# A graph layer on Trainium2: larger buffers for decoded counts and gathered rows, loads released by runs of six blocks, and counts copied out of PSUM by pairs of banks

## The chip, the cores and the metric

The kernel runs on one core of one Trainium2 chip. The metric is the device time of one execution in microseconds (us), as the median of several. Engines are named as in the profile: PE is TensorE (PEld are its weight loads, which run beside its products), DVE is VectorE, ACT is ScalarE, POOL is GpSimd, SP is SyncE, which here only issues DMAs. PSUM has eight banks of 2 KB per partition; a bank holds 512 columns of float32.

## The reference

A layer of a graph network with pre-normalization: 12500 nodes of 128 features, 200000 edges of four types, sorted by destination.

```python
h = maximum(layernorm(x), 0)                       # [12500, 128]
for i in range(4):
    msgs += where(edge_type == i, h[src] @ W[i] + b[i], 0)
out = x + segment_sum(msgs, dst, num_segments=12500)
```

The destinations are drawn as 12500 u² with u uniform, so low-numbered nodes have many edges and high-numbered ones few.

## The kernel before, in words

The edges lie in 1563 chunks of 128. Because matrix products are linear, rows of `h` are first added up by destination and type, and the sums are multiplied by `W` afterwards. The kernel does this adding in two ways.

**The dense side** takes the first 568 chunks, whose destinations have many edges. It does not fetch a row for each edge but counts, for a small set of destinations and types (a *unit*), how often each of the 12500 source nodes occurs, and multiplies the counts with the whole table of `h`. There are 580 units in 19 batches (22 in the first batch, 31 in each other).

- `count` builds one-hot matrices on DVE (L1068, L1076) and multiplies them on PE (L1101) into `pt`, one bank of the PSUM pool `x_ps` (four banks, L278 to L281 has the PSUM pools). When the last product of a unit is issued, the copy of `pt` to SBUF as int32 (`counts`, ACT, L1109) is put on the list `owed`; `settle(owed)` issues it, at the end of the next unit at the latest. Counts of three destinations are packed into the digits of one number.
- `multiply` takes the counts of the batch before through the table `dtab` in DRAM. The table is read in 33 parts of three blocks of 128 rows (288 KB each, SP, L1200, tiles `hs`, pool of STREAM = 5). Two parts (RUN = 2), six blocks, make a *run*. In a run six products take the undecoded counts (`c = 0`, L1215) and six take decoded ones (`c = 1`, L1207); the decoding is done by ACT (L1169) into tiles `dec` of three blocks, four of them (DECS = 4). All products of a batch add up in one bank `pa`. After each three products the generator yields. The first batch goes another way (L1226, L1237) and writes `dtab` (`keep`, L1183 to L1185).
- At the end of a batch ACT reads `pa` into `sd` (L1253), `tail` multiplies it with `W` (L1260, a bank of `x_ps`), and DVE adds the result to `acc` (L1279).

**The gather side** takes the other 995 chunks, in groups of 16. POOL fetches the 128 rows of a chunk by an indirect DMA (L590) into tiles `hm` of two chunks (HG = 2, pool `rows` of 10). DVE makes a one-hot matrix for each chunk (L608), `sum_up` adds rows by destination and type on PE (L643, three products a chunk, four chunks in one bank of `s_ps`, which has two), and ACT copies such a sum to `sb` (L633, put on the list `sums_owed` and issued when the next bank of `s_ps` is taken). Then `weigh` counts the edges for the bias with four products into `pc` (L660, a bank of `x_ps`), copies them (ACT, `cnt`, L664), and multiplies `cnt` and `sb` with the weights into `py` (L667, L669, pool `y_ps` of one); DVE adds `py` to a ring of results (L732). `prep_steps` prepares indices of 128 chunks with two transposes into `pg` (L375, L376), and `leave` (L765, L770) transposes results, adds x and writes them out.

**Order.** The main loop (L1561 to L1666) goes over the groups. In it PE, DVE and ACT run in the order in which the program writes their instructions; SP and POOL are ordered by their own queues. A group has eight parts of two chunks. After each part of `sum_up`, `pace` says how much of the dense work is due, and the loop takes so many steps of `dense_work`, which mixes `count` of batch n with `multiply` of batch n−1. At the second part the `py` step of the group before is issued, at the sixth the `pc` step of this group, and at other points steps of preparation and output. After the dense work is over (`dense_out`) the loop finishes the last groups and the output.

In PSUM, `x_ps` has four banks, `s_ps` two, `y_ps` one and `a_ps` (for `pa`) one: all eight.

Of the kernel before, what the change touches and what calls it, by code (L numbers as in the profile page):

```python
# [35 lines left out]
F32 = mybir.dt.float32  # L36
# [14 lines left out]
P = 128  # L51
EPS = 1e-5
UN = 3
G = 16
# [15 lines left out]
OT = 4  # L70
HG = 2
RAW = 3
LEAD = RAW
# [3 lines left out]
DS = 3  # L77
DECS = 4
RUN = 2
UP = 4096.0  # L80
# [7 lines left out]
def kernel(  # L88
# [189 lines left out]
    x_ps = mid.enter_context(tc.tile_pool(name="x_ps", bufs=4, space=PSUM))  # L278
    s_ps = mid.enter_context(tc.tile_pool(name="s_ps", bufs=2, space=PSUM))
    y_ps = mid.enter_context(tc.tile_pool(name="y_ps", bufs=1, space=PSUM))  # L280
    a_ps = mid.enter_context(tc.tile_pool(name="a_ps", bufs=1, space=PSUM))  # L281
    raw_room = ExitStack()
    aheads = raw_room.enter_context(tc.tile_pool(name="aheads", bufs=4))
# [233 lines left out]
    NU = len(spans)  # L517

    def load_span(u):
        j0, j1 = spans[u]  # L520
        xt = hpool.tile([P, HG * D3], F16, name="hm").bitcast(F32).rearrange("p (j d) -> p j d", d=D)
        load_nodes(xt, j0, j1)
        return xt
# [60 lines left out]
    def gather(t0, g):  # L584
        got = []
        for h0 in range(0, g, HG):
            hm = hpool.tile([P, HG * D3], F16, name="hm")
            for i in range(h0, min(h0 + HG, g)):
                at = (t0 + i) % (TURN * P)
                one = nc.gpsimd.indirect_dma_start(  # L590
                    out=hm[:, (i - h0) * D3 : (i - h0 + 1) * D3],
                    out_offset=None,
                    in_=htab,
                    in_offset=bass.IndirectOffsetOnAxis(ap=srcf[:, at : at + 1], axis=0),
                )
# [4 lines left out]
        return lambda i, c: of(got[i // HG], c)[:, (i % HG * 3 + c) * D : (i % HG * 3 + c + 1) * D]  # L600

# [13 lines left out]
    def settle(of):  # L615
        while of:
            of.pop(0)()

    adds = []
# [29 lines left out]
    def weigh(t0, g, oh, sb, last):  # L649
        win = window_of(C0 + t0)  # L650

        def bank(own):
            settle(owed)
            to = y_ps.tile([P, G * WIN], F32, name="py") if own else x_ps.tile([P, G * WIN], F32, name="pt")
# [10 lines left out]
        yield True  # L665
        py = bank(not last)
        nc.tensor.matmul(py[:, :g, :], b128, cnt[:, :g, :], start=True, stop=False)  # L667
# [88 lines left out]
    def leave(j0, j1, of, c0):  # L756

        nf = min(j1, N // P) - j0
        xt = seen_out.pop(j0) if j0 in seen_out else fetch(j0, j1)
        settle(owed)  # L760
        pt = x_ps.tile([P, OT, DO], F32, name="pt")
        for j in range(j0, j1):
# [12 lines left out]

        return rest

# [69 lines left out]
    def check_all():  # L847
# [4 lines left out]
        nc.vector.tensor_copy(many[:, 2:3], held)  # L852
        pb = x_ps.tile([P, 3], F32, name="pt")
        ones = outp.tile([P, P], F32, name="ones", bufs=1)
# [189 lines left out]
    def count(now, room):  # L1044
# [6 lines left out]
        order = sorted((n / len(of), i) for of in like.values() for n, i in enumerate(of))  # L1051
        for _, i in order:
            of = slots_of(vs[i])
# [37 lines left out]
        yield 0.0  # L1091
        counts = now[1] = room().tile([P, NW + 1, UB * NT], I32, name="counts")
        for n, of in enumerate(sets):
            supply(n)
            for k, (i, s, by, first, last) in enumerate(of):
# [3 lines left out]
                if first:  # L1099
                    pb = x_ps.tile([P, NB + NT], F32, name="pt")  # L1100
                one = nc.tensor.matmul(pb, o1, o2, start=first, stop=last)  # L1101
# [4 lines left out]
                if last:  # L1106
                    settle(owed)
                    owed.append(
                        lambda i=i, pb=pb: nc.scalar.copy(  # L1109
                            counts[:, :, i * NT : (i + 1) * NT], pb.rearrange("p (b t) -> p b t", t=NT)  # L1110
                        )
                    )
                done += 1
# [37 lines left out]
    def multiply(now):  # L1151
# [9 lines left out]
        parts = [(j0, min(j0 + HB, NW)) for j0 in range(0, NW, HB)]  # L1161
        decoded = {}

        def decode(n):
            j0, j1 = n * DS, min(n * DS + DS, NW)
            if first or j0 >= NW:
                return
            decoded[n] = decp.tile([P, DS, 3 * UB * NT], F32R, name="dec")
            nc.scalar.activation(  # L1169
# [8 lines left out]
        def keep(n, hs):  # L1178
            j0, j1 = parts[n]
            both = decp.tile([P, DS, 3 * UB * NT], F32R, name="dec").rearrange("p j v -> p (j v)")  # L1180
            both = both[:, : HB * D3 // 2].rearrange("p (j f) -> p j f", j=HB)[:, : j1 - j0]
# [12 lines left out]
        pa = a_ps.tile([P, 512], F32, name="pa")  # L1194
        to = pa[:, :nv]
        for n in range(0, 0 if first else len(parts), RUN):
            run = []
            for j0, j1 in parts[n : n + RUN]:
                hs = rooms[2].tile([P, HB, D3], F16, name="hs")
                nc.sync.dma_start(hs[:, : j1 - j0, :], table[:, j0:j1, :])  # L1200
                run += [(j, hs[:, j - j0, :]) for j in range(j0, j1)]
            for c in (0, 1):
                if n + RUN + c not in decoded:
                    decode(n + RUN + c)
                for j, row in run:
                    if c:
                        nc.tensor.matmul(  # L1207
                            to.rearrange("p (m v) -> p m v", m=3),
# [3 lines left out]
                            stop=(j == NW - 1),  # L1212
                        )
                    else:
# [41 lines left out]
        def tail(sd):  # L1256
            settle(owed)
            py = x_ps.tile([P, 3 * UB], F32, name="pt")
            for t in range(NT):
# [21 lines left out]

            tails.append(rest)

# [277 lines left out]
    for gi, (t0, g) in list(enumerate(zip(starts, sizes)))[RAW:]:  # L1561
# [56 lines left out]
        if work is None and not dense_out:  # L1618
# [178 lines left out]
```

## Time and profile before

| | |
|---|---|
| median of three runs | 1589.8 us (1585.2, 1589.8, 1591.06) |
| profiled execution | 1605.82 us, span 1604.1 us |
| granted PE clock, mean | 0.930 |
| busy: PE, ACT, DVE, POOL | 1317.4, 1077.8, 1004.4, 966.3 us |
| moved by DMA | 322.55 MB, 201 GB/s in the mean |
| count copies (L1109) | 580, 278.8 us |
| decodes (L1169) | 594, 662.2 us |
| gathers (L590) | 947, 915.0 us |

A row of a group reads: line, engine, operation, tile written <- tiles read, shapes, how many; then busy time in us and the mean of one in ns; then the idle time of the engine just before these instructions, and what ended it. A row of the timeline has start and duration in us; instructions of one line that follow each other closely are one row with their number (x6). In brackets stands the idle time before, and its releaser. "SPq" rows are DMA issues, "issue" is waiting for nothing that the profile shows, "remote" for something it cannot name. A row of the waits has who waited, the tile and line, for what, then the total in us, how many times, and the longest.

### The profile page before, as it was taken

What the parts mean: (1) busy time and instruction counts of PE and PEld (TensorE: products, weight loads), DVE (VectorE), ACT (ScalarE), POOL (GpSimd) and SP (SyncE); (2) the same over time, 40 slices, a digit from 0 to 9 for tenths busy, and PEclk for the clock granted to TensorE, in tenths of its full rate; (3) what the DMA queues carried; (4) which work ended last, traced back from release to release, by engine and by line L of the source; (5) the groups of instructions that cost most, each with busy time, mean ns of one, the idle gap of its engine ahead of it and who ended that gap; (6) DMA issues with size and microseconds to landing.
All of it is one profiled execution on the core that took longest, in us unless ns stands there. A gap on an engine that the chain in (4) does not pass through costs nothing.

```text
span 1604.1 us, 30332 instructions
## 1 busy us (share of the span) xinstructions
PE 1317.4 (82%) x9232; PEld 899.3 (56%) x9232; DVE 1004.4 (63%) x5138; ACT 1077.8 (67%) x1815; POOL 966.3 (60%) x1024
## 2 busy tenths in 40 slices
PE   4876876688889887988889888888888888888885
PEld 1334654466566665656556565665656565565654
DVE  7784466647677765766665575656656565666524
ACT  5675433577677776777677776877777777767651
POOL 6525566666666666666666665666666666666662
PEclk9885798799999999999999999999999999999997
DMA  7542398476676666667676765766666666656762
GB/s 210 186 168 69 113 294 279 123 240 216 192 219 211 216 200 204 209 206 225 190 228 207 227 212 183 229 200 213 216 215 201 207 207 202 215 187 209 254 190 74
DMA packets 184629, 322.55 MB, mean 201 GB/s; under 512 B 30243, under 2 KB 82524, under 8 KB 184460
## 3 DMA queue, kind: packets, MB, share of 16 engines
q1 hardware_dynamic: 132716, 214.63, 42.1%
q0 software_dynamic: 46992, 96.30, 20.0%
q10 hardware_dynamic: 4752, 9.64, 1.6%
q8 instruction: 73, 1.20, 0.3%
q14 instruction: 96, 0.79, 0.1%
HBM read 294.78 MB, written 25.67 MB: 200 GB/s over the span
## 4 chain that ended last, share of the span: by engine, by line
PE 64%; issue 10%; DMA 8%; ACT 7%; DVE 6%; another core or an unknown queue 4%; SPq 1%; DVEq 0%; ACTq 0%
PE pa L1207 16%; PE pa L1215 15%; PE pt L1101 10%; DMA hs<-dtab 7%; PE py L669 6%; PE ps L643 6%; ACT dec L1169 3%; PE pt L1260 2%; PE pa L1237 1%; ACT counts L1109 1%; DVE o L1068 1%; PE ps L701 1%; DVE o L1076 1%; DVE ring L732 1%
## 5 line engine op out<-in xcount | busy, mean ns | idle before, releaser
L590 POOL DMA_INDIRECT hm<-htab,srcT x947 | 915.0, 966 | 570.0 <-issue 207.0
L1169 ACT ACTIVATE dec<-counts 128x1116 fp32r<-128x1116 uint8 (+1 forms) x594 | 662.2, 1136 | 46.4 <-PE pa L1207 12.6
L1068 DVE TENSOR_SCALAR o<-iota_n,hkT 128x392 bf16<-128x392 f16 x1069 | 354.3, 331 | 387.1 <-PE pt L1101 184.6
L1215 PE MATMUL pa<-counts,hs 128*128 128x372 fp8e4 x1764 | 370.9, 336 | 80.6 <-DMA hs<-dtab 37.1
L1207 PE MATMUL pa<-dec,hs 128*128 128x372 f32 x1764 | 411.9, 364 | 29.6 <-ACT dec L1169 14.9
L1109 ACT CAST counts<-pt 128x396 int32<-128x396 f32 x580 | 278.8, 496 | 184.4 <-PE pt L1101 43.7
L1207 PEld LDWEIGHTS pa<-dec,hs 128*128 128x128 f32 x1764 | 309.0, 193 | 68.7 <-issue 30.1
L1101 PE MATMUL pt<-o,o 128*128 128x396 bf16 x1069 | 292.8, 344 | 53.7 <-issue 27.0
L1215 PEld LDWEIGHTS <-hs 128*128 128x128 f16 x1764 | 160.2, 99 | 234.4 <-issue 81.3
L1076 DVE TENSOR_SCALAR o<-iota_b,loT,byT 128x128 bf16<-128x128 bf16 x647 | 213.4, 330 | 0.0
L643 PE MATMUL ps<-oh,hm 128*128 128x72 bf16 (+7 forms) x2841 | 185.0, 201 | 26.6 <-issue 20.6
L643 PEld LDWEIGHTS <-hm 128*128 128x128 f16 x2841 | 149.4, 101 | 101.9 <-issue 54.4
L732 DVE TENSOR_TENSOR ring<-ring,py 128x18 f32 (+6 forms) x912 | 158.6, 174 | 58.4 <-issue 19.3
L608 DVE TENSOR_SCALAR oh<-iota_b,keyT 128x72 bf16<-128x72 bf16 (+7 forms) x947 | 161.8, 257 | 39.3 <-PE pa L1207 23.4
L633 ACT ACTIVATE sb<-ps 128x288 f32<-128x288 f32 (+8 forms) x237 | 99.5, 421 | 108.0 <-PE ps L643 32.2
L1101 PEld LDWEIGHTS <-o 128*128 128x128 bf16 x1069 | 86.6, 99 | 84.6 <-issue 31.2
L669 PE MATMUL py<-sb,wsb 128*128 128x288 f32 (+6 forms) x456 | 123.6, 414 | 0.8 <-issue 0.8
L1076 DVE TENSOR_SCALAR o<-iota_b,loT 128x128 bf16<-128x128 bf16 x422 | 121.7, 288 | 0.0
L669 PEld LDWEIGHTS py<-sb,wsb 128*128 128x128 f32 x456 | 84.1, 195 | 25.0 <-issue 3.9
L664 ACT CAST cnt<-pt 128x288 bf16<-128x288 f32 (+10 forms) x62 | 24.3, 393 | 96.8 <-remote 38.7
L574 POOL DMA_INDIRECT hx<-in_x_dram,srcT x48 | 46.1, 961 | 39.9 <-DVE varr L493 11.0
L1237 PE MATMUL pa<-counts,hs 128*128 128x264 fp8e4 x294 | 45.8, 300 | 11.9 <-DMA hs<-htab 7.1
(251 smaller groups left out, 804.1 us busy)
## 6 DMA issues: line engine op xcount, KB each, us to landing
hs<-dtab SPq DMA_DIRECT2D x576, 288.0 KB
hm<-htab,srcT POOLq DMA_INDIRECT x947
htab<-h SPq DMA_DIRECT2D x32, 288.0 KB
hs<-htab SPq DMA_DIRECT2D x32, 288.0 KB
dtab<-dec ACTq DMA_DIRECT2D x32, 288.0 KB
xo<-in_x_dram SPq DMA_DIRECT2D x23, 256.0 KB
out_dram<-xo SPq DMA_DIRECT2D x23, 256.0 KB
hm<-in_x_dram SPq DMA_DIRECT2D x18, 192.0 KB
```

What stands on the lines that cost most here:

```text
L590: one = nc.gpsimd.indirect_dma_start(out=hm[:, (i - h0) * D3 : (i - h0 + 1) * D3], out_offset=None, in_=htab, in_offset=bass.IndirectOffse ...
L608: nc.vector.tensor_scalar(oh[:, i, :], iota_b[:, :K], keyf[:, at : at + 1], None, ALU.is_equal)
L643: nc.tensor.matmul(ps[:, i - i0, :], rows(i, c), oh[:, i, :], start=(c == 0), stop=(c == 2))
L669: nc.tensor.matmul(py[:, :g, :], wsb[:, t, :], sb[0][:, :g, t, :], start=False, stop=(t == NT - 1))
L732: nc.vector.tensor_tensor(to, to, of(i), ALU.add)
L1068: one = nc.vector.tensor_scalar(o2[:, k, :NB], iota_n, hkT[:, s : s + 1], None, ALU.is_equal)
L1076: one = nc.vector.tensor_scalar(o1[:, k], iota_b, loT[:, s : s + 1], by, ALU.is_equal, ALU.mult)
L1101: one = nc.tensor.matmul(pb, o1, o2, start=first, stop=last)
L1109: lambda i=i, pb=pb: nc.scalar.copy(counts[:, :, i * NT : (i + 1) * NT], pb.rearrange("p (b t) -> p b t", t=NT))
L1169: nc.scalar.activation(decoded[n][:, : j1 - j0, :nv].rearrange("p j (m v) -> p j m v", m=3), by_digit[:, j0:j1, : nu * NT * 4].rearrange(" ...
L1207: nc.tensor.matmul(to.rearrange("p (m v) -> p m v", m=3), row.bitcast(F32R)[:, D // 2 :], decoded[j // DS][:, j % DS, :nv].rearrange("p (m ...
L1215: nc.tensor.matmul(to.rearrange("p (m v) -> p m v", m=3), row[:, :D], counts[:, j, : nu * NT * 4].rearrange("p (v m) -> p m v", m=4)[:, :3 ...
```

## The change

- Gathered rows: tiles `hm` hold four chunks (HU = 4) instead of two, and the pool has 5 tiles instead of 10. The gates that hold a gather back stay at every second chunk. `load_span`, used in the set-up, puts two spans into one tile.
- Decoded counts: a `dec` tile holds a run of six blocks, and there are two (DECS // RUN) instead of four; `half(n)` gives the half for part n, to `decode` and to `keep`.
- Table loads: the load of part n+i is held by the last `c = 1` product of the run in which the load five before it (STREAM) is used.
- Count copies: after the set-up the four single banks of `x_ps` are given up for `z_ps`, two tiles of two banks each. Two units are counted into one tile, one into each bank, and `keep_pair` copies both with one ACT instruction; a unit left over at a batch's end is copied alone.
- `pair()` hands out such a tile; it first issues every copy that is on `owed` and every reader that is on the new list `unadded`. `tail`, `pg` of `prep_steps` and, until `dense_out`, `leave` take a pair and use its first bank.
- `pc` takes its bank from `bank()`: until `dense_out` that is a bank of `s_ps`, after `settle(sums_owed)`. After `dense_out` the pairs are given up for four single banks again.
- The constant AHEAD is added and not used.

The diff without the parts that only rename:

```diff
-    hpool = mid.enter_context(tc.tile_pool(name="rows", bufs=10))
+    hpool = mid.enter_context(tc.tile_pool(name="rows", bufs=5))
...
-        settle(owed)
-        pg = x_ps.tile([P, 2, P], F32, name="pt")
+        pg = (bank() if dense_out else pair()[:, 0, :])[:, : 2 * P].rearrange("p (q e) -> p q e", q=2)
...
-        for h0 in range(0, g, HG):
-            hm = hpool.tile([P, HG * D3], F16, name="hm")
-            for i in range(h0, min(h0 + HG, g)):
+        for h0 in range(0, g, HU):
+            hm = hpool.tile([P, HU * D3], F16, name="hm")
+            for i in range(h0, min(h0 + HU, g)):
...
-                if i == h0 and gates and t0 + i >= SOON:
+                if i % HG == 0 and gates and t0 + i >= SOON:
...
+    unadded = []
+
+    def pair():
+        settle(owed)
+        settle(unadded)
+        return z_ps.tile([P, 2, 512], F32, name="pz")
+
+    def bank():
+        if dense_out:
+            return x_ps.tile([P, 512], F32, name="pt")
+        settle(sums_owed)
+        return s_ps.tile([P, 512], F32, name="ps")
...
-        pc = bank(False)
+        pc = bank_of(False)
...
+        def keep_pair(pz, us):
+            to = counts.rearrange("p b (i t) -> p i b t", t=NT)
+            to = to[:, us[0] : us[-1] + 1 : max(1, us[-1] - us[0])]
+            nc.scalar.copy(to, pz[:, : len(us), : NB + NT].rearrange("p m (b t) -> p m b t", t=NT))
...
                 if first:
-                    pb = x_ps.tile([P, NB + NT], F32, name="pt")
+                    m = place[i]
+                    if m % 2 == 0:
+                        two = [pair(), sorted(order[m : m + 2])]
+                    pb = two[0][:, two[1].index(i), : NB + NT]
...
-                    owed.append(
-                        lambda i=i, pb=pb: nc.scalar.copy(
-                            counts[:, :, i * NT : (i + 1) * NT], pb.rearrange("p (b t) -> p b t", t=NT)
-                        )
-                    )
+                    if m % 2 or m + 1 == len(order):
+                        owed.append(lambda two=two: keep_pair(*two))
...
+        def half(n):
+            if n % RUN == 0:
+                twin[:] = [decp.tile([P, RUN * DS, 3 * UB * NT], F32R, name="dec")]
+            return twin[0][:, n % RUN * DS : (n % RUN + 1) * DS, :]
...
-                nc.sync.dma_start(hs[:, : j1 - j0, :], table[:, j0:j1, :])
+                load = nc.sync.dma_start(hs[:, : j1 - j0, :], table[:, j0:j1, :])
+                by = (n + i - STREAM) // RUN
+                if by in last:
+                    held_by(load, last[by], "a run of blocks is multiplied as a whole")
...
-            settle(owed)
-            py = x_ps.tile([P, 3 * UB], F32, name="pt")
+            py = pair()[:, 0, : 3 * UB]
...
-            tails.append(rest)
+            unadded.append(rest)
+            tails.append(lambda: settle(unadded))
...
+    ahead_ps.close()
+    z_ps = ahead_ps.enter_context(tc.tile_pool(name="z_ps", bufs=2, space=PSUM))
...
-    decp = counting.enter_context(tc.tile_pool(name="decp", bufs=DECS, side="right"))
+    decp = counting.enter_context(tc.tile_pool(name="decp", bufs=DECS // RUN, side="right"))
...
             counting.close()
+            ahead_ps.close()
+            x_ps = ahead_ps.enter_context(tc.tile_pool(name="x2_ps", bufs=4, space=PSUM))
```

More of the change, by code (lines that the diff above doesn't have):

```diff
@@ L71 @@
 HG = 2
+HU = 4
 RAW = 3
@@ L78 @@
 DECS = 4
+AHEAD = 3
 RUN = 2
@@ L281 @@
     a_ps = mid.enter_context(tc.tile_pool(name="a_ps", bufs=1, space=PSUM))
+    ahead_ps = mid.enter_context(ExitStack())
+    x_ps = ahead_ps.enter_context(tc.tile_pool(name="x_ps", bufs=4, space=PSUM))
     raw_room = ExitStack()
@@ L517 @@
     NU = len(spans)
+    wide = []
     def load_span(u):
         j0, j1 = spans[u]
-        xt = hpool.tile([P, HG * D3], F16, name="hm").bitcast(F32).rearrange("p (j d) -> p j d", d=D)
+        if u % 2 == 0:
+            wide[:] = [hpool.tile([P, HU * D3], F16, name="hm").bitcast(F32).rearrange("p (u j d) -> p u j d", u=2, d=D)]
+        xt = wide[0][:, u % 2]
         load_nodes(xt, j0, j1)
@@ L650, in weigh, with bank_of @@
         win = window_of(C0 + t0)
-        def bank(own):
-            settle(owed)
-            to = y_ps.tile([P, G * WIN], F32, name="py") if own else x_ps.tile([P, G * WIN], F32, name="pt")
+        def bank_of(own):
+            to = y_ps.tile([P, G * WIN], F32, name="py") if own else bank()
             return to[:, : G * win].rearrange("p (g n) -> p g n", g=G)
         ohv = oh.rearrange("p g (t n) -> p g t n", t=NT)
-        pc = bank(False)
+        pc = bank_of(False)
         for t in range(NT):
@@ L665, in weigh @@
         yield True
-        py = bank(not last)
+        py = bank_of(not last)
         nc.tensor.matmul(py[:, :g, :], b128, cnt[:, :g, :], start=True, stop=False)
@@ L759, in leave @@
         xt = seen_out.pop(j0) if j0 in seen_out else fetch(j0, j1)
-        settle(owed)
-        pt = x_ps.tile([P, OT, DO], F32, name="pt")
+        pt = (bank() if dense_out else pair()[:, 0, :]).rearrange("p (j o) -> p j o", o=DO)
         for j in range(j0, j1):
@@ L774, in rest @@
                 nc.sync.dma_start(out[(j1 - 1) * P :, :], xt[: rows_of(j1 - 1), nf, :])
-        return rest
+        if dense_out:
+            return rest
+        todo = [rest]
+        unadded.append(lambda: settle(todo))
+        return lambda: settle(todo)
     def put_out(j0, j1, again):
@@ L852, in check_all @@
         nc.vector.tensor_copy(many[:, 2:3], held)
-        pb = x_ps.tile([P, 3], F32, name="pt")
+        pb = bank()[:, :3]
         ones = outp.tile([P, P], F32, name="ones", bufs=1)
@@ L1051, in count @@
         order = sorted((n / len(of), i) for of in like.values() for n, i in enumerate(of))
-        for _, i in order:
+        order = [i for _, i in order]
+        place = {i: m for m, i in enumerate(order)}
+        for i in order:
             of = slots_of(vs[i])
@@ L1167, in decode @@
                 return
-            decoded[n] = decp.tile([P, DS, 3 * UB * NT], F32R, name="dec")
+            decoded[n] = half(n)
             nc.scalar.activation(
@@ L1179, in keep @@
             j0, j1 = parts[n]
-            both = decp.tile([P, DS, 3 * UB * NT], F32R, name="dec").rearrange("p j v -> p (j v)")
+            both = half(n).rearrange("p j v -> p (j v)")
             both = both[:, : HB * D3 // 2].rearrange("p (j f) -> p j f", j=HB)[:, : j1 - j0]
@@ L1195, in multiply @@
         to = pa[:, :nv]
+        last = {}
         for n in range(0, 0 if first else len(parts), RUN):
             run = []
-            for j0, j1 in parts[n : n + RUN]:
+            for i, (j0, j1) in enumerate(parts[n : n + RUN]):
                 hs = rooms[2].tile([P, HB, D3], F16, name="hs")
-                nc.sync.dma_start(hs[:, : j1 - j0, :], table[:, j0:j1, :])
+                load = nc.sync.dma_start(hs[:, : j1 - j0, :], table[:, j0:j1, :])
+                by = (n + i - STREAM) // RUN
+                if by in last:
+                    held_by(load, last[by], "a run of blocks is multiplied as a whole")
                 run += [(j, hs[:, j - j0, :]) for j in range(j0, j1)]
@@ L1206, in multiply @@
                     if c:
-                        nc.tensor.matmul(
+                        last[n // RUN] = nc.tensor.matmul(
                             to.rearrange("p (m v) -> p m v", m=3),
@@ L1212, in multiply @@
                             stop=(j == NW - 1),
-                        )
+                        ).ins
                     else:
```

5 lines of the change are left out of this document (2 added, 3 removed).

## The prediction, made before the changed kernel had run

> **What bounds the kernel now.** I read the page's busy shares first, then the chain, then a table of windows, and last the waits.
>
> ```profile
> span 1604.1 us, 30332 instructions
> PE 1317.4 (82%) x9232; PEld 899.3 (56%) x9232; DVE 1004.4 (63%) x5138; ACT 1077.8 (67%) x1815; POOL 966.3 (60%) x1024
> ...
> PE 64%; issue 10%; DMA 8%; ACT 7%; DVE 6%; another core or an unknown queue 4%; SPq 1%; DVEq 0%; ACTq 0%
> PE pa L1207 16%; PE pa L1215 15%; PE pt L1101 10%; DMA hs<-dtab 7%; PE py L669 6%; PE ps L643 6%; ACT dec L1169 3%; PE pt L1260 2%; PE pa L1237 1%; ACT counts L1109 1%; DVE o L1068 1%; PE ps L701 1%; DVE o L1076 1%; DVE ring L732 1%
> ```
>
> ```profile
> 400.00:600.00 200.00, 174.75 (x1277) 122.88 (x1277) 138.68 (x717) 145.40 (x228) 125.02 (x130) 0.95 0.66 208
> ...
> sum 1000.00, PE 866.38 PEld 600.84 DVE 639.80 ACT 733.98 POOL 623.65; mean PE 173.28 PEld 120.17 DVE 127.96 ACT 146.80 POOL 124.73
> ```
>
> The first of five equal windows and the sum and mean of all five: from 400 to 1400 us the work is even, PE is busy 87% of the time, ACT 73%, POOL 62%. So PE sets the pace, in one written order, and what is left to win or lose is its 134 us of idle time in those 1000: short stops at which PE waits for a table load, for ACT, or for another engine.
>
> ```profile
> PEld L1215 <- DMA hs<-dtab: 64.2, 60, 2.8
> PE pt L1101 <- ACT counts L1109: 6.4, 4, 4.1
> PE pa L1215 <- DMA hs<-dtab: 37.1, 39, 2.4
> PEld pa L1207 <- ACT dec L1169: 24.6, 30, 3.0
> PE pa L1207 <- ACT dec L1169: 14.9, 20, 2.6
> ACT dec L1169 <- PE pa L1207: 12.6, 12, 2.2
> ```
>
> (Who waited, for what: us in total, times, longest. PEld and PE show the same stop twice, in part.) Table loads cost most; the count copies, of which the change makes most, cost PE four waits. The change adds no arithmetic to PE, so its effect is in such waits.
>
> **The change, part by part.** I sum against the profiled execution (1605.82 us, 1.0% above the median of 1589.8), and carry the difference over to the median.
>
> *1. Counts copied by pairs of banks.* 580 units are copied one by one now; after, 281 pairs and 18 single ones, 299 copies.
>
> ```profile
> L1109 ACT CAST counts<-pt 128x396 int32<-128x396 f32 x580 | 278.8, 496 | 184.4 <-PE pt L1101 43.7
> L633 ACT ACTIVATE sb<-ps 128x288 f32<-128x288 f32 x36 | 15.0, 417 | 15.6 <-PE pt L1101 4.7 <-PE py L669 4.7 <-PE ps L643 3.5
> L633 ACT ACTIVATE sb<-ps 128x384 f32<-128x384 f32 x28 | 13.8, 492 | 11.2 <-PE ps L643 4.4 <-PE pt L1101 2.6 <-PE py L669 1.6
> ...
> 924.12 0.88 ACT L1109 CAST counts<-pt 128x396 int32<-128x396 f32 x2 [1.64 <-PE pt L1101]
> ```
>
> No copy of 792 columns exists before. The two L633 forms differ by 75 ns over 96 columns, 0.78 ns a column, so a pair takes 496 + 396 x 0.78 = 805 ns. Against two copies apart (992) this saves 0.19 us, against two back to back (0.88) 0.07: 281 x that is 20 to 53 us of ACT. ACT is idle over a quarter of the time, and the PE waits on ACT listed above come to some 46 us; a lighter ACT can shorten those only in part. I take -16, ends 0 and -53, nearer to the small end because the chain gives these copies 1%. The Trainium skill (Perfetto Trace Analysis, section "Optimizing Scalar/DVE Operations") says that grouping pays when the engine is saturated, and that where it is not, but makes others wait, breaking instructions up may let work finish sooner. The windows show ACT unsaturated; by that rule the -16 falls away and the sum below would be 1674.
>
> *2. Slack of those banks.* Today four banks turn, so a bank's copy may take until four units later; with two pairs the copy of a pair begins when the second unit is counted and must be done two units on. It ends 0.31 us (805 - 496) later than the second unit's copy did. If every pair showed this, 281 x 0.31 = 87 us; if none, 0. The present row (4 waits in 580) is nearest to none: +8.
>
> *3. Others that take a pair.* 19 `tail`s, 7 transposes `pg` and 19 `leave`s, 45 in all, now occupy a pair, and each allocation first issues every copy that is owed; the next count pair finds both pairs just used. The trace's own example of PE going PE to ACT and back without slack is the end of a batch, where `pa` must be read into `sd` (L1253) before the next batch's first L1215:
>
> ```profile
> 916.08 0.61 PE L1207 MATMUL pa<-dec,hs 128*128 128x372 f32 x2
> 919.70 0.48 ACT L1253 ACTIVATE sd<-pa 128x372 f32<-128x372 f32 x1
> 920.23 1.15 PE L1215 MATMUL pa<-counts,hs 128*128 128x372 fp8e4 x6 [1.07 <-ACT dec L1169]
> ```
>
> The last product ends at 916.69, ACT reads 3.0 us later, PE goes on at 920.23 after 1.07 us of idleness (it had other work for the rest). 45 x 1.07 = 48 us is the high end, 0 the low one; most of these have two pairs' time, so +5.
>
> *4. `pc` in the banks of the sums.* The counts of edges (`pc`, L660, 4 matmuls a group) leave the four single banks and take one of the two `ps` banks. Order of PSUM in a group: sum 1 in A, 2 in B, 3 in A, `pc` in B, sum 4 in A. So sum 4 (L643) waits for the copy of sum 3 (L633), which `bank()` issues immediately ahead of `pc`. Today `pc` has a bank of its own, sum 4 takes the other `ps` bank, free since long, and the copy of sum 3 comes on ACT right behind `cnt` (L664). Where ACT stands at that moment is seen in the trace:
>
> ```profile
> 910.29 0.43 PE L660 MATMUL pt<-oh,three 128*32 128x288 bf16 x4
> 910.77 0.40 ACT L664 CAST cnt<-pt 128x288 bf16<-128x288 f32 x1 [1.18 <-PE pt L660]
> ...
> 933.24 0.31 PE L660 MATMUL pt<-oh,three 128*32 128x288 bf16 x4
> 935.72 0.41 ACT L664 CAST cnt<-pt 128x288 bf16<-128x288 f32 x1
> ...
> 1082.21 0.32 PE L660 MATMUL pt<-oh,three 128*32 128x320 bf16 x4
> 1085.76 0.43 ACT L664 CAST cnt<-pt 128x320 bf16<-128x320 f32 x1
> ...
> 1105.62 0.32 PE L660 MATMUL pt<-oh,three 128*32 128x320 bf16 x4
> 1110.72 0.45 ACT L664 CAST cnt<-pt 128x320 bf16<-128x320 f32 x1
> ```
>
> In the first group ACT had waited for `pc`, so the copy would be over by 910.01: no stall. In the others ACT comes free (no idle time in front of `cnt`) 2.2, 3.2 and 4.8 us after `pc` ended, and a copy of 0.42 comes on top: 2.6, 3.6, 5.2 us that PE would stand, with the counts, the products and everything else queued behind sum 4. The same subtraction over the 57 groups up to the last decode,
>
> ```profile
> 169.22 0.35 PE L660 MATMUL pt<-oh,three 128*32 128x192 bf16 x4
> 169.92 0.34 ACT L664 CAST cnt<-pt 128x192 bf16<-128x192 f32 x1
> ...
> 1548.21 0.35 PE L660 MATMUL pt<-oh,three 128*32 128x384 bf16 x4
> 1552.71 0.48 ACT L664 CAST cnt<-pt 128x384 bf16<-128x384 f32 x1 [4.31 <-remote]
> ```
>
> (the first and the last) gives a median of 2.2 us and 126 us in all. A stop lets ACT and the loads get ahead, so later stops shrink; the round trip without slack that the trace does have costs 1.07. I take 57 x 1.07 = +61, ends 0 and +126. This is the largest term, and it is a wait on PE where none is now.
>
> *5. Loads tied to ends of six blocks.* A table load (L1200) waits for the room of a load five back. Today the first load of a run is released after 3 products of L1207, the second after 6; after, both by the sixth, three matmuls later.
>
> ```profile
> SPq L1200 <- PE pa L1207: 294.9, 117, 7.0
> ...
> 914.16 1.32 PE L1207 MATMUL pa<-dec,hs 128*128 128x372 f32 x6
> 924.51 0.83 SPq L1200 DMA_DIRECT2D hs<-dtab  x2
> 928.57 0.83 SPq L1200 DMA_DIRECT2D hs<-dtab  x2
> ```
>
> SP is mostly waiting (for L1207 alone 295 us) and issues the loads in twos already, every 4.06 us here. Six products take 1.32 us, the first three half of it, so the earlier release is lost by about 0.6 us, one load in two. The 39 to 60 stops on `hs` would each grow by that: 23 to 36 us; 288 runs x 0.6 = 173 is the far end, 0 the near one, because step 4's stops give loads time. What stands behind a held load on SP (loads of x and of indices) waits as long, none with a PE wait above. I take +8.
>
> *6. Decoded counts in one tile of six blocks.* The first decode of a run waits for six products of the run before last instead of three, 0.6 us later again; ACT waits for that 12 times now. Ends 0 and 2 x 12.6 = 25; +2.
>
> *7. Gathered rows by four chunks.* Same room, fewer releases; the last rows of a tile come free up to two chunks later.
>
> ```profile
> L590 POOL DMA_INDIRECT hm<-htab,srcT x947 | 915.0, 966 | 570.0 <-issue 207.0
> 905.78 0.94 POOL L590 DMA_INDIRECT hm<-htab,srcT  x1 [0.30 <-issue]
> PE ps L643 <- DMA hm<-htab,srcT: 0.9, 2, 0.5
> ```
>
> A gather with its issue is 1.24 us, 16 of them 20 us, a group lasts 23 (`pc` at 910.29 and at 933.24), and PE waited for rows twice: the idle time of POOL covers it, 0. Without that cover, two chunks a group at 1.24 us would be at most 2.5 x 57 = 141; nothing speaks for it. Fewer updates of semaphores by PE come with steps 1, 5 and 7 (281, about 288 and about 237 fewer).
>
> ```profile
> L1215 PE MATMUL pa<-counts,hs x1764: 325/326/535, 298.1 to 1551.4; 128*128 128x372 fp8e4 x196
> L1207 PE MATMUL pa<-dec,hs x1764: 325/333/775, 300.2 to 1554.6; 128*128 128x372 f32 x196
> ```
>
> L1207 carries such an update at every third product, L1215 hardly any; the medians differ by 7 ns, 1764 x 7 = 12 us in all. I take 0, the other end -12. The Trainium skill (TensorE: Matmul & The Clock Gate, section "The cost: per-tile semaphore tail") has increments of packed tiles one after another at about 26 ns each; an estimate by it, 806 x 26 ns, would be -21 and the sum 1637. No run here shows that.
>
> Sum: -16 + 8 + 5 + 61 + 8 + 2 + 0 = +68, so 1605.8 + 68 = 1674 for a profiled execution, and 1589.8 + 68 = **1658** for the median.
>
> **The rivals.**
> - *Faster: the new stops come out of old ones.* PE is idle 134 us in 1000 anyway, and the 126 us of step 4 use ACT's present place, which itself is late in places because PE has just run ahead. If after a stop ACT and the loads are ahead, the table waits shrink by as much, and ACT's 20 to 53 us are left: middle -30, **1560**. It decides where, with the terms of steps 2, 3, 5 and 6 at their zero ends, the round trip costs under 0.4 us net a group: 22 of the 30 us over 57 groups, 8 us being 0.5%. For: one of the four groups shown would not stop. Against: three would, by over 2 us, and the `hs` waits are not caused by ACT.
> - *No change:* the stops of step 4 are hidden too, and the +7 of the other terms is all that is left, less than can be told, **1590** to 1597.
> - *Slower by the loads:* step 4 is hidden, but the tie holds: stops on `hs` at a third of the 288 runs grow by 0.6 us, 58 us, less 16: **1632**. For: these waits are PE's costliest. Against: the rows show loads going in twos already.
>
> **How the numbers follow.** My forecast, 0.53, with its own range 1620 to 1720 (half of the round trip to most of the 126). Faster 0.28; no change 0.07; by the loads 0.12. A change under 0.5% can't be told here, the three runs of before lie 0.4% apart. Slower: 0.53 + 0.12 = 0.65. The range must reach down into the faster case: from 1552 (the far ends of step 1 and of the updates, below it, are left out, some 0.1) to 1725 (step 4 at its high end with +9 for the rest; above it some 0.08).
>
> **What would show it.** In the profile after, a row PE `ps` waiting for ACT `sb` of 40 to 130 us shows step 4 (no such row is among the longer waits now); without it my forecast is wrong. 299 count copies near 0.8 us show step 1; PE waiting for ACT counts above 20 us would show that step 2 or 3 is undersized; waits for `hs` above 130 us (64.2 and 37.1 now) step 5; PE waiting for gathered rows step 7. If ACT's idle time grows while PE's falls, the faster rival was right.

## The result: 3.3% slower, and the profile after

The median of five runs is 1653.88 us (1632.46 to 1662.95) against 1589.8 us before. The ratio leaves out two slow runs (1658.49 and 1662.95 us) and is therefore smaller than the quotient of these medians. It is 1.0334, with a 95% interval of 1.0269 to 1.0398, or about +53 us. The profiled execution took 1653.88 us, 48 us more than the one of before.

The page of the changed kernel: busy shares, the first part of its chain by line, and the groups of the count copies and of the count products.

```profile
span 1652.2 us, 29542 instructions
...
PE 1317.1 (80%) x9232; PEld 922.9 (56%) x9232; DVE 1003.3 (61%) x5138; ACT 1065.4 (64%) x1534; POOL 969.4 (59%) x1024
...
PE 62%; ACT 11%; issue 8%; DMA 6%; another core or an unknown queue 5%; DVE 5%; POOL 1%; SPq 1%; ACTq 0%; DVEq 0%; POOLq 0%
...
L1133 PE MATMUL pz<-o,o 128*128 128x396 bf16 x1069 | 304.7, 355 | 94.6 <-ACT counts L1120 50.3
...
L1120 ACT CAST counts<-pz 128x792 int32<-128x792 f32 (+1 forms) x299 | 238.4, 799 | 140.6 <-PE pz L1133 64.0
```

PE and ACT do the same work as before or less: PE 1317.1 us against 1317.4, ACT 1065.4 against 1077.8. The span grew by idle time alone. The mean granted clock was lower, 0.907 against 0.930, but two products of one line follow each other as before (in both traces 165 ns from start to start in the median with undecoded counts, 171 ns with decoded ones), so the clock is not what made the difference. In the chain ACT went from 7% to 11%, DMA from 8% to 6%: the chain now runs over ACT more often. The waits show where (line 662 is the sum of gathered rows, 652 its copy, 1133 the counts, 1120 their copies, 1254 and 1246 the products with undecoded and decoded counts, 1298 the tail, 1204 the decoding):

```profile
PE ps L662 <- ACT sb L652: 52.2, 28, 6.4
PE pz L1133 <- ACT counts L1120: 50.3, 30, 5.2
PEld L1254 <- DMA hs<-dtab: 41.8, 35, 2.7
ACT dec L1204 <- PE pa L1246: 39.6, 37, 3.4
PE pa L1254 <- DMA hs<-dtab: 27.7, 27, 2.3
PEld pz L1298 <- ACT counts L1120: 19.3, 8, 5.7
PE pz L1298 <- ACT counts L1120: 16.1, 5, 5.0
```

Three new stops of PE for ACT stand here: the fourth sum for the copy of the third (52.2 us), counts for count copies (6.4 before, 50.3 now), tails for count copies. Against that the stops for table loads fell (64.2 and 37.1 before, 41.8 and 27.7 now), and the rows of PE waiting for decoded counts (24.6 and 14.9 before) are not among the longer waits any more.

To compare kernels I summed in each trace by how much the start of one PE instruction follows the start of the one before it later than their usual spacing (gaps over 60 ns, from 300 us to the last product with decoded counts), by kind of instruction:

```
gaps of PE, us         before  after  e1_pc_only  e3_singles  e4_releases
all                     323.1  371.0       323.3       351.9        341.5
fourth sums of groups     5.5   90.8       128.7        85.8          5.2
counts, for ACT or DVE   36.6   61.2        17.5        31.0         36.5
tails, for ACT            1.2   13.3         0.9         0.9          0.7
c = 0, for table loads   71.8   43.5        33.4        77.8        102.1
c = 1, for ACT           27.6    5.8         6.6         6.3         12.0
```

All gaps grew by 47.9 us, as much as the two profiled executions differ. The parts do not add up in a simple way: 85 us of new stops at the sums came, and 50 us of old ones at the table loads and decoded counts went. The row of the fourth sums has all gaps there, also those that the view of waits puts down to something other than ACT. And the execution traced of before, 1605.82 us, lies 16 us above the median of its own runs and 22 us above the one beside e1 to e4. Differences from its column are uncertain by about as much.

### The profile page after: what moved, and what is told of

Its sections match the earlier page's. It is cut to its first block, busy times and chain, and to the rows that moved or that the text cites. A ratio compares the mean times of both kernels' runs of the same rounds, so it can differ in the third digit from the quotient of the medians.

```text
span 1652.2 us, 29542 instructions
## 1 busy us (share of the span) xinstructions
PE 1317.1 (80%) x9232; PEld 922.9 (56%) x9232; DVE 1003.3 (61%) x5138; ACT 1065.4 (64%) x1534; POOL 969.4 (59%) x1024
## 4 chain that ended last, share of the span: by engine, by line
PE 62%; ACT 11%; issue 8%; DMA 6%; another core or an unknown queue 5%; DVE 5%; POOL 1%; SPq 1%; ACTq 0%; DVEq 0%; POOLq 0%
PE pa L1246 16%; PE pa L1254 14%; PE pz L1133 11%; PE py L687 6%; PE ps L662 5%; ACT dec L1204 5%; DMA hs<-dtab 4%; ACT counts L1120 3%; PE pz L1298 2%; PE pt L975 1%; POOL hm L596 1%; PE pa L1276 1%; PE ps L678 1%; ACT sb L652 1%
## 5 line engine op out<-in xcount | busy, mean ns | idle before, releaser
L1246 PE MATMUL pa<-dec,hs 128*128 128x372 f32 x1764 | 416.3, 371 | 6.9 <-issue 3.9
L1254 PE MATMUL pa<-counts,hs 128*128 128x372 fp8e4 x1764 | 366.1, 338 | 40.9 <-DMA hs<-dtab 27.7
L1133 PE MATMUL pz<-o,o 128*128 128x396 bf16 x1069 | 304.7, 355 | 94.6 <-ACT counts L1120 50.3
L1246 PEld LDWEIGHTS pa<-dec,hs 128*128 128x128 f32 x1764 | 322.2, 200 | 33.3 <-issue 14.7
L1120 ACT CAST counts<-pz 128x792 int32<-128x792 f32 (+1 forms) x299 | 238.4, 799 | 140.6 <-PE pz L1133 64.0
L1254 PEld LDWEIGHTS <-hs 128*128 128x128 f16 x1764 | 166.0, 100 | 213.8 <-issue 78.7
L662 PE MATMUL ps<-oh,hm 128*128 128x72 bf16 (+7 forms) x2841 | 183.0, 203 | 87.8 <-ACT sb L652 52.2
L662 PEld LDWEIGHTS <-hm 128*128 128x128 f16 x2841 | 154.5, 102 | 155.7 <-issue 109.8
L1099 DVE TENSOR_SCALAR o<-iota_b,loT 128x128 bf16<-128x128 bf16 x422 | 117.4, 278 | 0.0
L682 ACT CAST cnt<-ps 128x288 bf16<-128x288 f32 (+7 forms) x58 | 23.0, 396 | 43.7 <-remote 19.6
```

Source lines behind the costliest of these rows:

```text
L662: nc.tensor.matmul(ps[:, i - i0, :], rows(i, c), oh[:, i, :], start=(c == 0), stop=(c == 2))
L1099: one = nc.vector.tensor_scalar(o1[:, k], iota_b, loT[:, s : s + 1], by, ALU.is_equal, ALU.mult)
L1120: nc.scalar.copy(to, pz[:, : len(us), : NB + NT].rearrange("p m (b t) -> p m b t", t=NT))
L1246: last[n // RUN] = nc.tensor.matmul(to.rearrange("p (m v) -> p m v", m=3), row.bitcast(F32R)[:, D // 2 :], decoded[j // DS][:, j % DS, :nv ...
L1254: nc.tensor.matmul(to.rearrange("p (m v) -> p m v", m=3), row[:, :D], counts[:, j, : nu * NT * 4].rearrange("p (v m) -> p m v", m=4)[:, :3 ...
```

## The experiments

The kernel before ran beside each of these on the same chip, and each ratio is against that. Beside e1 to e4 it took 1583.8 us; beside e5 to e8 it took 1346.6 us and beside e9 to e12 1347.8 us, the same kernel on another, faster chip. What differs there is told in the last section. The trace of before that this document shows comes from a run at 1606 us; its time places it with the slower chip, so it is set beside traces of that chip only.

### e1: the edge counts alone

```diff
             settle(owed)
+            if not own and not dense_out:
+                settle(sums_owed)
+                return s_ps.tile([P, 512], F32, name="ps")[:, : G * win]...
             to = ... if own else x_ps.tile([P, G * WIN], F32, name="pt")
```

(In the kernel before, nothing else changed. It still issues the owed count copies ahead of `pc`, by `settle(owed)`; the changed kernel no longer does so there, so its stop at the sums need not be as long as here.)

> The kernel before with one edit: the edge counts `pc` take a bank of the sums, everything else (single count copies in four banks, releases, buffers) as before. My theory: the fourth sum of a group waits for the copy of the third, so this alone costs +55 to +85 us, 1645 to 1675, and the row PE `ps` waiting for ACT `sb` shows 50 us or more. Rival, the pairs of banks cost most and this stop is absorbed: under +20, 1590 to 1610. Rival, table loads: no change, 1590.

Measured: 1594.96 us, ratio 1.0076 (1.0049 to 1.0104), about +12 us. The waits of this run (643 the sums, 1218 and 1210 the products):

```profile
PE ps L643 <- ACT sb L633: 81.3, 29, 5.8
PE ps L643 <- DMA hm<-htab,srcT: 17.5, 8, 3.8
PEld L1218 <- DMA hs<-dtab: 28.2, 32, 2.2
PE pa L1218 <- DMA hs<-dtab: 14.9, 16, 1.8
PE pa L1210 <- ACT dec L1172: 4.7, 8, 1.6
```

The stop is there: 81.3 us by this view, and by the table of gaps 123 us more ahead of the fourth sums, near the high end of the prediction (126); of these the view puts 17.5 us down to gathered rows. But the time rose by 12 us. The stops for table loads fell from 37.1 to 14.9 us and those for decoded counts from 14.9 to 4.7, and all gaps of PE together are what they were (323). That fits this account: while PE stands for one thing, the loads and ACT get ahead, and PE does not stand for them afterwards. The price is shown by the times; where the stops went rests on one pair of traces, and loads also went out less late in this one than in that of before (last section). My theory of +55 to +85 us falls: the stop came, and its price did not.

### e2: the copy of the third sum issued earlier

```diff
                 if spent is None:
                     work = None
+                if j == max(0, parts - 3) and not dense_out:
+                    settle(sums_owed)
```

> The changed kernel with one edit: the copy of a group's third sum is issued after the first dense step of its part, so that it stands on ACT about 3 us ahead of `pc`. My theory: most of the wait of the fourth sum goes, 60 us or so of the 64, and what the pairs cost (some 13) and their lighter ACT are left: 1590 to 1615. Rival, pairs: at most -20 us against the changed kernel, 1635 or more. A third way: ACT now stands and waits for the third sum and delays decodes, so that half is given back: 1615 to 1635.

Measured: 1639.85 us, ratio 1.0328 (1.0267 to 1.0389), not to be told from the changed kernel's 1.0334.

```profile
PE ps L662 <- ACT sb L652: 14.1, 12, 2.2
PEld L1254 <- DMA hs<-dtab: 62.8, 58, 3.9
PE pz L1133 <- ACT counts L1120: 47.5, 29, 5.7
PE pa L1254 <- DMA hs<-dtab: 37.2, 40, 3.3
```

The stop at the sums shrank from 52.2 to 14.1 us, and the waits for table loads rose from 27.7 to 37.2 (PE) and from 41.8 to 62.8 (weight loads). This is the same exchange as in e1, the other way round: taking most of this stop away bought nothing that can be told, where my theory had 1590 to 1615 us. The 1635 or more of the rival (pairs) came, but this run does not show that the pairs are the reason.

### e3 and e11: the pairs undone

```diff
-    z_ps = ...tile_pool(name="z_ps", bufs=2, space=PSUM)
+    z_ps = ...tile_pool(name="z_ps", bufs=4, space=PSUM)
...
-        return z_ps.tile([P, 2, 512], F32, name="pz")
+        return z_ps.tile([P, 1, 512], F32, name="pz")
...
-                    if m % 2 == 0:
-                        two = [pair(), sorted(order[m : m + 2])]
+                    two = [z_ps.tile([P, 1, 512], F32, name="pz"), [i]]
...
-                    if m % 2 or m + 1 == len(order):
-                        owed.append(lambda two=two: keep_pair(*two))
+                    owed.append(lambda two=two: keep_pair(*two))
```

(In the changed kernel; the readers of tails and outputs are issued as before, too.)

> The changed kernel with the pairs undone: each unit in a bank of its own out of four, copied by itself, tails and transposes in one bank; `pc` in the sums' banks, tied loads, larger buffers stay. My theory: the pairs' net is small (terms +8, +5, -16), so the time stays within 20 us of the changed kernel, 1635 to 1675. Rival, pairs cost most: near 1600.

Measured: 1627.57 us, ratio 1.0226 (1.0123 to 1.0329), which overlaps with the changed kernel's. So it was run again on the faster chip, beside the changed kernel itself (e9).

> The changed kernel with the pairs undone, as before (single banks, single copies; pc, ties and buffers as changed), beside the changed kernel itself. Theory: the pairs cost more by their shorter slack than their lighter ACT gives: 10 to 25 us under the changed kernel on the slower chip, 0 to 10 on the faster. Rival, prediction: pairs give about 3 us net, so it is 0 to 5 us above the changed kernel.

Measured: 1375.87 us, ratio 1.0197 (1.0162 to 1.0232), against 1388.81 and 1.0294 (1.0261 to 1.0328) for the changed kernel: the intervals lie apart, and the pairs cost 12.9 us, 1.0%. The waits of e11, and then of e9:

```profile
PE pz L1128 <- ACT counts L1116: 5.0, 5, 1.2
```

```profile
PE pz L1133 <- ACT counts L1120: 21.0, 24, 1.4
PE pz L1298 <- ACT counts L1120: 3.3, 7, 0.9
```

The difference in these rows, 16 us for the counts and some 2 for the tails, is about the price. ACT has 13 us less to do with pairs, 1054.9 us in e9 against 1067.9 in e11, and the kernel is slower all the same. First e9, then e11:

```profile
PE 1238.4 (89%) x9232; PEld 882.4 (63%) x9232; DVE 999.3 (72%) x5138; ACT 1054.9 (76%) x1534; POOL 972.6 (70%) x1024
```

```profile
PE 1229.5 (89%) x9232; PEld 881.2 (64%) x9232; DVE 995.5 (72%) x5138; ACT 1067.9 (78%) x1815; POOL 975.8 (71%) x1024
```

The rival (pairs) is right in sign here; by size it is a third of the whole.

### e4: the three releases, without the changes in PSUM

The kernel before with the tied loads, the tiles of six blocks and the rows by four, each as in the diff of the change.

> The kernel before with the releases alone: tied table loads, decoded counts in tiles of six blocks, gathered rows in tiles of four chunks; PSUM and copies as before. My theory: terms +8, +2 and 0, so 1590 to 1610. Rival, the tied loads cost most: +40 or more, 1630 and up, with the waits for `hs` grown by 30 us. Rival, fewer updates by PE help: 1565 to 1580.

Measured: 1613.11 us, ratio 1.0176 (1.0128 to 1.0225), about +28 us.

```profile
PEld L1230 <- DMA hs<-dtab: 116.8, 88, 3.3
PE pa L1230 <- DMA hs<-dtab: 79.5, 64, 2.9
ACT dec L1180 <- PE pa L1222: 25.8, 23, 2.8
```

The stops for table loads doubled, 37.1 to 79.5 us on PE. That is more than my theory gave, and less than the rival's +40. With e1 it accounts for e3 within its interval: 0.8% and 1.8% against 2.3% (1.2 to 3.3).

### e5, e6, e7: each release by itself

Each is the kernel before with one of the three edits. The ties:

```diff
-                nc.sync.dma_start(hs[:, : j1 - j0, :], table[:, j0:j1, :])
+                load = nc.sync.dma_start(hs[:, : j1 - j0, :], table[:, j0:j1, :])
+                by = (n + i - STREAM) // RUN
+                if by in last:
+                    held_by(load, last[by], "a run of blocks is multiplied as a whole")
...
-                        nc.tensor.matmul(
+                        last[n // RUN] = nc.tensor.matmul(
...
-                        )
+                        ).ins
```

> The kernel before with the tied table loads alone. The three releases together cost 1.8% (28 us). My theory now: the stream of table loads sets the pace, and the tie, which takes half a run of lead from every second load, is nearly all of it: +18 to +30 us, waits of L1215-products for `hs` 25 us or more above the kernel before. Rival, the tiles of decoded counts: under +8 here.

Measured: 1364.08 us, ratio 1.0120 (1.0092 to 1.0149), about +17 us, just under the 18 to 30 of my theory.

The tiles of six blocks:

```diff
+        def half(n):
...
-            decoded[n] = decp.tile([P, DS, 3 * UB * NT], F32R, name="dec")
+            decoded[n] = half(n)
...
-    decp = ...tile_pool(name="decp", bufs=DECS, side="right")
+    decp = ...tile_pool(name="decp", bufs=DECS // RUN, side="right")
```

> The kernel before with decoded counts in two tiles of six blocks, alone. My theory (ties): under +8 us, ACT waiting for PE's L1207 some 10 us longer than before. Rival (decoded counts): +15 to +30, because each second decode begins half a run later and ACT, behind it, comes late for the copies.

Measured: 1351.69 us, ratio 1.0030 (1.0009 to 1.0050), about +5 us.

The gathered rows:

```diff
-    hpool = mid.enter_context(tc.tile_pool(name="rows", bufs=10))
+    hpool = mid.enter_context(tc.tile_pool(name="rows", bufs=5))
...
-            hm = hpool.tile([P, HG * D3], F16, name="hm")
+            hm = hpool.tile([P, HU * D3], F16, name="hm")
...
```

> The kernel before with gathered rows in five tiles of four chunks, alone. My theory and the prediction: no change, within 0.5%. Rival (rows): +10 us or more, with PE waiting for `hm`. A third way, fewer updates by PE: -5 to -15.

Measured: 1341.73 us, ratio 0.9966 (0.9949 to 0.9984), about 5 us faster.

The waits for table loads and of the decoding, first with the ties alone, then with the tiles alone, then with the rows alone:

```profile
PE pa L1219 <- DMA hs<-dtab: 34.5, 45, 2.1
ACT dec L1169 <- PE pa L1211: 6.5, 8, 1.9
```

```profile
ACT dec L1175 <- PE pa L1213: 21.1, 23, 1.9
PE pa L1221 <- DMA hs<-dtab: 14.7, 28, 1.3
```

```profile
PE pa L1220 <- DMA hs<-dtab: 21.9, 28, 2.0
ACT dec L1174 <- PE pa L1212: 6.9, 7, 3.5
```

There is no trace of the kernel before from this chip, so the three are read against each other. The ties are most of it: PE waits 34.5 us for loads with them, 14.7 and 21.9 without. With the tiles of six ACT waits 21.1 us for PE instead of 6.5 or 6.9, and the time rises by 5. Why rows by four chunks gain 0.3% isn't shown. PE has some 200 updates of its semaphore less to make (1851 of its instructions carry one in the trace of e7, 2052 in that of e6). The Trainium skill (TensorE: Matmul & The Clock Gate, section "The cost: per-tile semaphore tail") has about 26 ns for each increment of packed tiles; an estimate by it, 200 updates of 26 ns, would be 5 us. That agrees in size, but the run doesn't show that this is the cause.

### e8 and e12: one more tile for table loads

```diff
-STREAM = 5
+STREAM = 6
...
-    hpool = mid.enter_context(tc.tile_pool(name="rows", bufs=10))
+    hpool = mid.enter_context(tc.tile_pool(name="rows", bufs=9))
```

> The kernel before with six tiles for table loads instead of five (STREAM = 6), and nine tiles of gathered rows instead of ten, to make room. If the lead of the table loads sets the pace, as the theory now says, one more tile takes the waits for `hs` from some 70 to under 25 us and the time falls by 15 to 40 us, to 1545 to 1570. Rival: PE's stops are handed on to the next wait (ACT), as they were when `pc` was moved, and the time falls by less than 8.

Measured: 1336.79 us, ratio 0.9920 (0.9891 to 0.9949), 10 us faster than the kernel before.

```profile
PE pa L1215 <- DMA hs<-dtab: 0.6, 2, 0.3
```

The waits for table loads are gone (0.6 us), and the time falls by less than the theory's 15 and more than the rival's 8. So the short lead of the loads costs time here, and one more tile gives 0.8% back. e12 joins it with rows by four chunks (four tiles of four):

> The kernel before with six tiles for table loads and four tiles of four chunks for gathered rows (the two edits that were faster alone, 0.8% and 0.3%). Theory: the lead of the loads is what PE waits for, so 0.9 to 1.2% faster than before on the faster chip, and 1 to 3% on the slower one, where loads are issued late. Rival: sixteen chunks of rows are too few ahead, and PE waits for `hm`, no gain.

Measured: 1337.28 us, ratio 0.9913 (0.9882 to 0.9944). It beats both kernels on that chip, but the 0.3% of e7 doesn't come on top of e8. Neither was tried on the slower chip.

### e9 and e10: the changed kernel on the faster chip, with and without ties

> The changed kernel as it is, beside the kernel before on the chip of this call. Two chips were seen: one on which before takes about 1585 us and the table loads are issued up to 5 us after the product that releases them, and one on which it takes about 1346 us and they are issued at once. Theory: the new waits are round trips between PE and ACT, so on the first the ratio is 1.03 again, and on the second 1.01 to 1.02, since the ties cost 1.2% there and gathered rows by four gave 0.3%. Rival, the costs do not depend on such delays: 1.03 on both.

Measured: 1388.81 us, ratio 1.0294 (1.0261 to 1.0328). The rival was right: the loss is 3% on both chips.

```diff
-                by = (n + i - STREAM) // RUN
-                if by in last:
-                    held_by(load, last[by], "a run of blocks is multiplied as a whole")
```

> The changed kernel without the ties of the table loads (each load again released by its own three products). Theory: what the ties cost alone (1.2%) comes back: 12 to 20 us under the changed kernel of the same call. Rival, the stops of `pc` and of the pairs already give the loads their time, so the ties cost nothing in the changed kernel: within 5 us of it.

Measured: 1379.62 us, ratio 1.0230 (1.0195 to 1.0264), 9 us under e9. That lies between theory (12 to 20) and rival (under 5), and the intervals just touch. Waits for table loads, e9 and then e10:

```profile
PE pa L1254 <- DMA hs<-dtab: 17.3, 24, 2.3
```

```profile
PE pa L1251 <- DMA hs<-dtab: 6.9, 8, 1.9
```

The waits for loads shrink by 10 us, as the time does. Alone the ties cost 17, in the changed kernel 9. A likely reason, not shown by a run, is that the stops for ACT give part of the lead back that the ties take.

## Why the prediction was right in its sum and wrong in most of its terms

The forecast was slower, +68 us, 1658 us; the measured ratio makes it +53, some 1643 us. The waits that it named as new appeared. But that the sum came so near is luck: errors of up to 49 us in its terms cancel.

| step of the prediction | forecast | measured |
|---|---|---|
| 4, `pc` in the banks of the sums | +61 | +12 (e1) |
| 5 to 7, the releases together | +10 | +28 (e4); on the faster chip 1.2%, 0.3% and -0.3% (e5 to e7) |
| 1 to 3, pairs of banks | -3 | 1.0%, +13 on the faster chip (e9 and e11) |

- *Step 4* named the right mechanism and the right raw stop: 126 us at the high end, 123 us more in the gaps of e1. The failed step is "57 x 1.07 = +61", that about half of the raw stop would be absorbed. Nine tenths were: in the traces PE's stops for loads and decoded counts shrank instead. The faster rival's argument, that new stops come out of old ones, was nearly right here. The share is not a constant, though: on the faster chip the view shows only 25.5 us of this stop (e11), and by subtraction (2.0% for e11 less 1.2% for the releases) `pc` costs about as much there, 0.8%, known to half a per cent.
- *Step 5* was undersized. I gave +8, with 23 to 36 us as the sum of the grown stops; the releases cost 28 together on the slower chip, and the ties alone are 1.2% on the faster. The row on which I went down, that loads go in twos already, was of one place; what counted, as I read it now, was that the wait for loads is the largest stop of PE.
- *Steps 1 to 3*: the copy was sized rightly (805 ns forecast; 299 copies take 238.4 us, with 18 single ones of 0.5 us this is 0.82 us a pair). ACT's relief was sized too high: the busy time of the copies fell by 40 us (278.8 to 238.4), but that of ACT by 12 (1077.8 to 1065.4), or 13 from e11 to e9, where the forecast had 20 to 53. The slack that the pairs take (forecast +8 and +5) costs more than this relief gives: 1.0% net instead of -3 us. The two were not measured apart. The rule of the Trainium skill (Perfetto Trace Analysis, section "Optimizing Scalar/DVE Operations") that breaking instructions up may let work finish sooner on an engine that is not saturated, weighed in step 1, agrees with e11: ACT is busy 78% of the time there, and single copies are 1.0% faster.
- *Steps 6 and 7* (+2 and 0) were within 5 us of what e6 and e7 measured. The count of updates in step 7 was too high: 675 fewer of PE's instructions carry one in the changed kernel (1376 against 2051), not 806.
- *The rivals.* That the tie alone makes the kernel slower held in part: ties are the largest single part on the faster chip, not the whole. Faster and no change did not come: what step 4 lost in price the releases and the pairs made up.

The parts add up: 1.2% and 0.3% less 0.3% for the releases (e5 to e7), 1.0% for the pairs (e9 and e11), 0.8% for `pc` (e1, on the other chip), together 3.0%, against 2.9% in e9 and 3.3% on the slower chip. That the parts add up in time while their waits exchange with each other is an observation; a model that gives each part's price from its stop is still lacking.

## What to carry to other kernels

A stop of PE that a trace shows, even one sized exactly, isn't its price: in a loop in which PE also stops for transfers and for another engine, a new stop can pay off old ones (123 us of new gaps, 12 us of time in e1), while of a change that takes lead from the transfer PE already waits for, more was paid (42 us more of PE's waits for loads, 28 us of time in e4). Before sizing a new wait by its length, ask which of the present waits in the same stretch would end earlier meanwhile. And making an engine lighter that is not the bound need not pay, when its larger instruction holds buffers for longer: the pairs took 13 us off ACT's busy time and added 1% to the whole.

## What was not expected of the hardware

The same kernel before took 1583.8 us on one chip and 1346.6 to 1347.8 us on another. The granted clock differs by some per cent: 0.91 to 0.93 in the profiled executions on the slower, 0.95 to 0.96 on the faster. PE's gaps differ by more: all together 323 us in the trace of before, 126 us in that of e6, which runs within 0.5% of before. That is 197 of the 253 us between their spans (1604.1 and 1350.9). The rows of SP show one difference: what the table loads (L1200 in before, L1206 in e6) were waiting for when they were issued. First before on the slower chip, then e6 on the faster:

```profile
SPq L1200 <- PE pa L1207: 294.9, 117, 7.0
SPq L1200 <- PE pt L1101: 253.7, 118, 7.9
SPq L1200 <- PE ps L643: 186.7, 73, 17.0
```

```profile
SPq L1206 <- PE pa L1213: 668.2, 274, 10.3
SPq L1206 <- PE pt L1101: 47.5, 99, 2.7
```

On the faster chip nearly every load goes out directly behind the product that releases it: 0.03 us after its end, in nine of ten loads that had waited. In the trace of before the median is 1.8 us and one in ten comes over 4 us late, behind other instructions of PE, to which the view then attributes it. In the other five traces of the slower chip the median is 0.6 to 1.1 us (0.9 in e1). The recorded updates of PE's semaphore point the same way: in e6, 97% of them come within 0.02 us of the end of a product that makes one, in the trace of before 23%, and one in ten comes over 1.9 us behind. So in these traces PE's signals come late on the slower chip. Whether the signals of the other engines do, and why, isn't settled; no run was made for it. The raw stop at the sums differs with the chip (90.8 us in the gaps of the changed kernel on the slower, 28.6 in e9 on the faster), while the loss in per cent was the same on both within the intervals. The granted clock of the changed kernel was not lower on the faster chip (0.962 to 0.965 in e9, 0.956 to 0.963 beside it), which also speaks against the clock as the cause of the loss.
